# A transformer block's preparation reordered: the condition turned by TensorE, the scale's product before the first turn, key products by part, fillings of zeros regrouped

## The chip, the cores and the metric

The kernel runs on one core of a Trainium2 chip. The metric is the device time of one execution in microseconds. Before the change the median of three runs is 727.88 us (727.65 to 728.49). TensorE (PE) multiplies matrices into PSUM banks; VectorE (DVE), ScalarE (ACT) and GpSimd (POOL) work on tiles of 128 partitions; SyncE (SP) only issues DMA transfers. Each engine takes its instructions in the order in which the program has them and waits on semaphores of the others.

## The reference

The block works on 16 images of 256 tokens with 256 features. A condition vector per image gives shifts, scales and gates; self-attention, cross-attention with a context and an MLP follow, each with a residual.

```python
c_proj = jax.nn.silu(c) @ W_mod + b_mod
shift_a, scale_a, gate_a, shift_m, scale_m, gate_m = jnp.split(c_proj, 6, axis=-1)
x_norm = modulate(_ln(x), shift_a, scale_a)          # t * (1 + scale) + shift
q, k, v = jnp.split(x_norm @ W_qkv + b_qkv, 3, axis=-1)     # 16 heads of 16
attn_w = jax.nn.softmax(jnp.einsum('bhqd,bhkd->bhqk', q, k) * scale, axis=-1)
x = x + gate_a[:, None] * (merge(attn_w @ v) @ W_proj + b_proj)
...                                  # cross-attention with _ln(x) and _ln(context)
h = jax.nn.gelu(modulate(_ln(x), shift_m, scale_m) @ W_mlp1 + b_mlp1)
x = x + gate_m[:, None] * (h @ W_mlp2 + b_mlp2)
```

## The kernel before

The program has 32 *units*: the self-attention (s) of each of the 16 images and its cross-attention (c). For each unit a layernorm `xn` is made, turned by TensorE into feature-major form (`psT`), and multiplied with the weights into keys, queries and values (`ps_k`, `ps_q`, `psv`). Numbers are kept to nearly full float32 by splitting: a value is rounded to the type fp32r (its *high* part, `xTh`, `h_k`, `h_q`) and the rest is kept as a *low* part (`xTl`, `l_k`, `l_q`); a product of two such values is three products, high by high, weight high by low, weight low by high. The helper `mm3` issues these three for each of the two 128-feature halves of the inner dimension, interleaved, so the second of its six instructions already needs the low part. Keys and queries, high twice and low once, are copied by DMA into a *stack* `big` (three buffers, one per unit in flight, one half for queries and one for keys), from which the attention scores are products `st` and `s`. Rows of `big` that no copy writes must be zero; filling them with zeros is one word of the preparation for each half, done by GpSimd (a memset) or by ScalarE (a copy of the zero tile `wz`).

After the attention scores start, a fixed plan of *beats* sets what each engine does next to the two score products. Before it comes the *preparation*, which loads the weights, computes what the condition gives, and brings the first two units through keys and queries. The order of the preparation is written out by hand, as a list of words in the entry `PRE` of the table `E_`; each word is a function that issues instructions on one or more engines, and since every engine keeps program order, the list is the order on every engine. The words that the change and the prediction speak of:

- `load`: the first DMA loads, on SyncE in this order: one block of `W_mod` (for the scale), the bias rows `brow`, the key block of `W_qkv`, the shift's block of `W_mod`, the query block, input `x` of image 1, the value block. The condition `c_sb` is loaded ahead of them, the input of image 0 by ScalarE's queue. `ld2` loads the input of image 2; `lg`, `lc`, `lp` load the gate's, the cross projection's (`wcp_f`) and the projection's (`wp_f`) weights and biases.
- `L0a`, `L0b`, `L0d`: statistics of image 0 (VectorE `st_s`), their aggregate `mv_s` with the root on GpSimd (`rs_s`), and `xn_s` on VectorE. `L1a` to `L1d` are the same for image 1.
- `silu`, `turn`: tanh of half the condition on ScalarE (16 partitions by 256), the product `th` = (tanh + 1) c on VectorE, then TensorE turns `th` and ScalarE halves it into `sT` (128 by 32).
- `scale`, `sc1`, `shift`: eight TensorE instructions each (they show as `st<-sT,wf`), and a bias addition on VectorE into `cpT`; `sc1` adds 1 to the scale.
- `T0t`, `T0h`, `T0l`: the turn of image 0's `xn_s`, its scaled high part on ScalarE (needs `sc1`), its low part on VectorE.
- `brow`, `bp`, `bro2`: the bias rows turned, the odd rows copied on ScalarE and turned, and copied out.
- `hik`, `lok`, `hiq`, `loq`, `hiv`, `lov`: high part of a weight (ScalarE cast into `wself`) and its low part (GpSimd; for v VectorE).
- `K0a`, `K0m`: the first and second six instructions of unit 0's key product. `K0h`, `K0l`: `h_k` and `l_k`. `bk`, `bq`, `bv`: the biases that the shift adds (`st<-cpT,wf`, eight instructions, then `bqkv` on VectorE). `h_k` needs `bqkv`.
- `K0x`, `K0yp`, `K0w` and the same for Q: the three copies into the stack, on SyncE or, with p, on GpSimd's queue.
- `b15` and other `b` with a number: so many 128x128 products of zeros (*fillings* of TensorE, `s<-wz`), two instructions each, whose result nobody reads.
- `z0kp`, `z0qp`, `z1kp`: zeros into the key or query half of buffer 0 or 1 on GpSimd; `z1qa`: on ScalarE. `one0`: two rows of ones into buffer 0 by SyncE.

The first score product (`st<-big`) waits for all six copies of unit 0's stack.

Of the kernel before, what the change touches and what calls it, by code (L numbers as in the profile page):

```python
# [21 lines left out]
def pixart_block(  # L22
# [8 lines left out]
    B, N, H = x.shape  # L31
# [4 lines left out]
    KC = H // P  # L36
# [15 lines left out]
                return tc.keep_in_program_order(i) if self.on else i  # L52
            return issue

    E_ = {'CUT': 8, 'LN': {'s': 'pool', 'c': 'pool', 'q': 'pool'}, 'ON': (1, 1, 1), 'L0': -16, 'L1': 1, 'S0': -7, 'A0': 0, 'T0': 1, 'S1': 5, 'A1': 7, 'L2': 9, 'T1': 9, 'S2': 32, 'AP': 99, 'DV': (0, 1), 'HP': (1, 0), 'BZ': {}, 'AV': {1: [(1, 2), (1, 3)], 9: [(0, 0), (0, 1)]}, 'AHEAD': (0, 0, 0, 0, 0, 2), 'TW': {(21, 6): 'cb', (23, 5): 'u0', (23, 7): 'u1', (25, 2): 'u2', (27, 3): 'u3', (27, 7): 'h2a', (28, 0): 'l2 h0p u5', (28, 2): 'h1p', (28, 4): 'h3p', (28, 7): 'u4 u6', (29, 0): 'l3d', (29, 1): 'l0', (29, 2): 'l1', (29, 7): 'h5p', (30, 1): 'u7 h6d h7p', (30, 3): 'h4p', (31, 1): 'l4 l6d', (31, 2): 'l5d x2', (31, 4): 'l7', (31, 7): 'b2'}, 'BE': 'G0 av P g0 A1 G1 G2 N1 F7 g1 S0 PF s2 p2 G3 a2 aT aL G4 x3 b3 S1 S2 T2 C r0 G5 S3 G6 S4 s3 CF x4 F8 g2 G7 S5 F9 p3 S6 G8 a3 r1 G9 F10 G10 T3 g3 b4 x5 x6 S7 s4 F11 S8 S9 F12 G11 p4 a4 F13 r2 S10 G12', 'XP': 1, 'IL': 1, 'MF': 0, 'SH': 4, 'RAMP': 1, 'HA': 1, 'MP': 16, 'W': (7, 1, 0, 0), 'PRE': 'load L0a z0kp z0qp L0b silu b15 hik turn L0d brow bp z1qa lok T0t lg scale b1 lc sc1 bro2 T0h T0l shift b3 ld2 one0 hiq loq L1a hiv K0a L1b bk K0m L1d bq K0h K0l Q0a L2a T1t T1h lp K0yp K0x z1kp Q0m T1l bv K1a Q0h K0w Q0x Q0yp Q0l lov K1b Q1a Q0w L2b Q1b K1l V0a K1y Q1l z2ka ld3', 'SL': {(-1, 0): 'V0b wm one1 L2c', (-1, 1): 'V1a T2t T2h', (-1, 2): 'K1wp T2p', (-1, 3): 'K1xp L3a Q1yp V1b ga', (-1, 4): 'M0 z2qa Q1xp Q1wp pb L3b vone gs', (-1, 5): 'mods0 ld4', (-1, 6): 'K2a K2m L3p', (-1, 7): 'L3c cb lx gm', (0, 0): 'sp3 mods1', (0, 1): 'sp0', (0, 3): 'sp1', (0, 4): 'sc2', (0, 6): 'one2', (1, 1): 'sp2', (1, 2): 'sp4'}}

    PE = InOrder(nc.tensor, True)
    ACT, DVE, POOL, SP = (InOrder(e, True) for e in (nc.scalar, nc.vector, nc.gpsimd, nc.sync))

    const = ctx.enter_context(tc.tile_pool(name="const", bufs=1))  # L60
    work = ctx.enter_context(tc.tile_pool(name="work", bufs=2))
# [18 lines left out]
    ident = const.tile([P, P], F32, name="ident")  # L80
# [15 lines left out]

    BMOD, BQKV, BKVC, BM1 = 0, 12, 20, 24
    BQ, BK, BQC, BKC = 32, 34, 36, 38
    c_sb, th = [work.tile([B, 2, H], F32, tag=t, name=n, bufs=3)[:, 0] for t, n in (("qkh", "c_sb"), ("qkl", "th"))]
    SP.dma_start(c_sb, cond)  # L100
    X = {}

# [7 lines left out]
    brow = const.tile([32, P], F32, name="brow")  # L110
# [26 lines left out]
    sc1 = const.tile([P, 2, 2, B], F32, name="sc1")  # L137
    bT = const.tile([P, 40], F32, name="bT")
    sT = const.tile([P, KC, B], F32, name="sT")
    cb = const.tile([P, H], F32, name="cb")  # L140
# [43 lines left out]

    def f_silu():
        ACT.activation(dummy, mhalf, AF.Tanh)
        ACT.activation(th, c_sb, AF.Tanh, scale=0.5)
        DVE.scalar_tensor_tensor(th, th, 1.0, c_sb, ALU.add, ALU.mult)

    def f_turn():  # L190
        pst = st[:, 1, 480:]
        for k in range(KC):
            PE.transpose(pst[:, k * B:(k + 1) * B], th[:, k * P:(k + 1) * P], ident[:B, :B])
        ACT.mul(sT.rearrange("p k b -> p (k b)"), pst[:, :KC * B], 0.5)

    odd_rows = []

# [100 lines left out]
    wm = []  # L298
# [9 lines left out]
    gm = []  # L308
# [20 lines left out]
    def layernorm(src, name):  # L329
# [193 lines left out]
    def to_stack(W, src, bias, dst, which, name):  # L523

        o = Box()
        lo_row = (2, 1)[which]

        o.W, o.src, o.tok, o.name = W, src, False, name  # L530

        def first():
            o.ps = ps_gen(f"ps_{name}", LONG)
            mm3(o.ps[:, 0:N], W, 0, src.xT)

        def third():
            mm3(o.ps[:, N:], W, 1, src.xT)

        def second():
            third()  # L540
            high()

        def high():
            o.hi = work.tile([P, KC, N], F32R, tag="qkh", name=f"h_{name}", bufs=3)
            for f in range(KC):
                ACT.activation(o.hi[:, f], o.ps[:, f * N:(f + 1) * N], AF.Identity, bias=bias[f])

        def low():
# [496 lines left out]
    u0, u1 = units[:2]  # L1045
# [17 lines left out]
    for n, v in (("0", u0), ("1", u1), ("2", u2)):  # L1063
        word["T" + n + "t"], word["T" + n + "h"], word["T" + n + "l"] = v.T[0].parts
        word["T" + n + "p"] = v.T[0].low_pool
        for c in "KQ":
            o = getattr(v, c)
            word[c + n + "l"] = o.parts[2]
            word[c + n + "m"], word[c + n + "h"] = o.third, o.high
            word[c + n + "p"] = o.low_pool  # L1070
            for q, k in enumerate("xyw"):
                word[f"{c}{n}{k}"] = lambda o=o, q=q: o.send(q)
                word[f"{c}{n}{k}p"] = lambda o=o, q=q: o.send(q, POOL)
# [20 lines left out]
    u3 = units[3]  # L1094
# [3 lines left out]
    for i in range(5):  # L1098
        word[f"sp{i}"] = lambda i=i: f_split(i)
    word["vone"] = lambda: [POOL.memset(v[:, :, :, HD:], 1.0) for v in vts]  # L1100
    for n, f in (("load", f_load), ("silu", f_silu), ("turn", f_turn), ("brow", f_brow), ("bp", f_bp), ("bro2", f_bro2),
                 ("scale", f_scale), ("sc1", f_sc1), ("shift", f_shift),
                 ("lg", f_loads_g), ("lp", f_loads_p), ("lc", f_loads_c), ("lx", f_loads_x),
                 ("ga", f_ga), ("pb", f_pb), ("gs", f_gs), ("cb", f_cb),
                 ("wm", f_wm), ("mods0", lambda: f_mods(0)), ("mods1", lambda: f_mods(1)), ("sc2", f_sc2), ("gm", f_gm)):
        word[n] = f
# [9 lines left out]
    for i in range(3):  # L1116
        b = i if i < 2 else 0
# [159 lines left out]
    last, o, q = units[-1], units[-1].post, units[-2].post  # L1277
# [103 lines left out]
```

## Time and profile before

| | before |
|---|---|
| median of 3 runs | 727.88 us |
| lowest, highest | 727.65, 728.49 us |
| the profiled execution, its own time | 728.29 us |
| its span, first to last instruction | 726.5 us |
| TensorE busy | 718.9 us, 99% |
| TensorE's share of the chain that ended last | 93% |
| mean granted TensorE clock | 0.997 |

The span is 1.8 us shorter than the execution's own time. Busy time alone doesn't tell what counts: fillings count as busy, and so do products that wait for nothing but are early. The chain of waits is followed back from the last instruction; at each step it goes to what released the instruction or to the one before it on its engine. In rows of engines, the first number is the start in us, the second the duration, then come engine, line, operation, the tiles written and read, their shapes, how many instructions the row holds, and in brackets the idle time before it with what ended it. All recorded operations have the line of the recording helper, L51, so the tiles' names tell them apart.

### The profile page before, as it was taken

The numbers are of one execution on the slowest core, as the hardware profiler recorded it, in microseconds if no ns is written. First come the engines' busy times: TensorE is split into PE (matmuls) and PEld (weight loads), VectorE is DVE, ScalarE is ACT, GpSimd is POOL, SyncE is SP. The second block draws the span as 40 slices with busy tenths as digits, with TensorE's granted clock in tenths as the row PEclk, the third lists the DMA queues.
The fourth block names the chain that finished last, engine by engine and source line by source line (L and its number), as shares of the span: only waits on it lengthen the run. The fifth ranks groups of instructions, "written<-read, shape, count | busy, mean of one in ns | idle before, by whom it ended". The sixth has DMA issues, their size and how long they took to land.

```text
span 726.5 us, 24914 instructions
## 1 busy us (share of the span) xinstructions
PE 718.9 (99%) x10086; PEld 633.3 (87%) x10086; DVE 567.8 (78%) x1208; ACT 579.3 (80%) x1006; POOL 526.8 (73%) x561
## 2 busy tenths in 40 slices
PE   9999999999999999999999999999999999999997
PEld 8788888888888888888888888888878999999997
DVE  4888898989888888888889888888845675676552
ACT  5578898888888888888888888898887677777773
POOL 6766687969687786969687898979746756656643
PEclk9999999999999999999999999999999999999999
DMA  6645333332424343342433444244311414334421
GB/s 208 209 150 176 119 120 143 138 120 105 162 107 161 124 152 124 120 147 112 169 119 137 152 149 161 106 145 142 128 52 54 117 46 117 96 87 111 102 64 39
DMA packets 67110, 90.56 MB, mean 125 GB/s; under 512 B 6194, under 2 KB 38740, under 8 KB 66996
## 3 DMA queue, kind: packets, MB, share of 16 engines
q1 hardware_dynamic: 66164, 86.88, 35.8%
q8 instruction: 80, 1.31, 0.7%
q0 software_dynamic: 560, 1.84, 0.7%
q14 instruction: 34, 0.28, 0.1%
q10 hardware_dynamic: 272, 0.26, 0.1%
HBM read 26.97 MB, written 8.46 MB: 49 GB/s over the span
## 4 chain that ended last, share of the span: by engine, by line
PE 93%; POOL 3%; issue 1%; DVE 1%; ACT 1%; DMA 0%; POOLq 0%; ACTq 0%
PE s L51 18%; PE o L51 16%; PE st L51 15%; PE ph L51 10%; PE ps_P_s L51 4%; PE ps_qc L51 4%; PE ps_v_c L51 4%; PE ps_kc L51 4%; PE ps_q L51 4%; PE ps_v_s L51 3%; PE ps_k L51 3%; PE ps_P_c L51 2%; PE psT_q L51 1%; PE psA_s L51 1%; POOL hl L51 1%
## 5 line engine op out<-in xcount | busy, mean ns | idle before, releaser
L51 DVE TENSOR_REDUCE mx<-s 128x2 f32<-128x512 f32 x504 | 324.7, 683 | 64.3 <-PE s L51 59.0
L51 ACT ACTIVATE pt<-st 128x1024 f32<-128x1024 f32 x252 | 258.9, 1028 | 16.9 <-PE st L51 10.5
L51 PE MATMUL s<-big 63*128 63x256 f32 (+1 forms) x1024 | 185.6, 299 | 0.2
L51 PEld LDWEIGHTS s<-big 63*128 63x128 f32 (+1 forms) x1024 | 133.5, 186 | 19.1 <-DVE l_kc L51 6.6
L51 PE MATMUL st<-big 64*128 64x256 f32 (+1 forms) x1024 | 134.4, 299 | 0.5 <-DMA big<-l_q 0.3
L51 POOL TENSOR_TENSOR hl<-hf,hh 128x512 fp32r<-128x512 f32 x64 | 87.4, 1368 | 63.2 <-ACT hh L51 63.1
L51 PE MATMUL o<-pt,v 128*32 128x256 f32 x2048 | 123.8, 382 | 0.0
L51 PEld LDWEIGHTS st<-big 64*128 64x128 f32 (+1 forms) x1024 | 96.3, 187 | 16.0 <-issue 13.0
L51 PEld LDWEIGHTS o<-pt,v 128*32 128x32 f32 x2048 | 60.0, 109 | 41.4
L51 PE MATMUL ph<-wcross,wself 128*128 128x256 f32 x672 | 85.4, 277 | 0.0
L51 PEld LDWEIGHTS ph<-wcross,wself 128*128 128x128 f32 x672 | 80.4, 188 | 0.0
L51 ACT COPY oT<-o 128x512 f32<-128x512 f32 x63 | 37.0, 587 | 32.7 <-PE o L51 32.7
L51 ACT ACTIVATE hf<-ph,bT 128x256 f32<-128x256 f32 x114 | 47.7, 472 | 18.4 <-PE ph L51 18.4
L51 ACT ACTIVATE hh<-ph,bT 128x256 fp32r<-128x256 f32 x114 | 47.9, 473 | 17.9 <-PE s L51 8.7
L51 PE MATMUL ps_kc<-xTh_c,wcross 64*128 64x256 f32 x256 | 46.6, 291 | 0.0
L51 PE MATMUL s<-big,hh 128*128 128x256 f32 x256 | 45.2, 277 | 0.0
L51 PE MATMUL st<-big,hh 128*128 128x256 f32 x256 | 45.2, 277 | 0.0
L51 PE MATMUL ps_v_c<-wcross,xTh_c 64*128 64x256 f32 x256 | 44.3, 292 | 0.0
L51 PE MATMUL ps_k<-xTh_s,wself 64*128 64x256 f32 (+1 forms) x232 | 43.5, 293 | 0.0
L51 PE MATMUL ps_qc<-xTh_q,wcross 64*128 64x256 f32 x256 | 41.2, 280 | 0.0
L51 PE MATMUL ps_q<-xTh_s,wself 64*128 64x256 f32 (+1 forms) x240 | 40.7, 287 | 0.0
L51 POOL TENSOR_SCALAR xn_c<-c,mv_c,rs_c 128x256 f32<-128x256 f32 x32 | 39.0, 1227 | 1.7
(240 smaller groups left out, 2135.7 us busy)
## 6 DMA issues: line engine op xcount, KB each, us to landing
big<-h_kc SPq DMA_DIRECT2D x32, 256.0 KB
big<-h_qc SPq DMA_DIRECT2D x32, 256.0 KB
big<-h_k SPq DMA_DIRECT2D x30, 256.0 KB
big<-h_q SPq DMA_DIRECT2D x29, 256.0 KB
g<-gd SPq DMA_DIRECT2D x16, 256.0 KB
c<-in_ctx_dram SPq DMA_DIRECT2D x16, 256.0 KB
big<-l_kc SPq DMA_DIRECT2D x16, 256.0 KB
big<-l_qc SPq DMA_DIRECT2D x16, 256.0 KB
```

The source lines that it names most:

```text
L51: i = f(*a, **k)
```

## The change

Four edits, all in the preparation.

1. The condition is turned first: TensorE turns `c_sb` itself, inside `silu`; ScalarE takes from PSUM the tanh of half of it and half of it, both 128 by 32; a new word `th2` multiplies them on VectorE straight into `sT`. `turn` goes.
2. `scale` stands before the turn of image 0 (`T0t`); `shift` behind the first part of the key product.
3. Unit 0's key product is issued by parts: `K0i` all four high-by-high instructions for both output halves, `K0j` the four with the input's low part and then the four with the weight's low part.
4. Fillings: 15 + 1 + 3 products become 5 + 3 + 1 + 1, at other places; the zeros of buffer 0's query half go from GpSimd (`z0qp`) to ScalarE (`z0qa`).

The list moves with it: the load of image 2 goes ahead of the gate's weights, the projection weights (`lc`, `lp`) behind `h_k` and `l_k`, and statistics of image 2 behind `l_q`.

```diff
-    c_sb, th = [work.tile([B, 2, H], F32, tag=t, name=n, bufs=3)[:, 0] for t, n in (("qkh", "c_sb"), ("qkl", "th"))]
+    c_sb, th = [work.tile([p, 2, H], F32, tag=t, name=n, bufs=3)[:, 0]
+                for p, t, n in ((B, "qkh", "c_sb"), (P, "qkl", "th"))]
...
     def f_silu():
         ACT.activation(dummy, mhalf, AF.Tanh)
-        ACT.activation(th, c_sb, AF.Tanh, scale=0.5)
-        DVE.scalar_tensor_tensor(th, th, 1.0, c_sb, ALU.add, ALU.mult)
-
-    def f_turn():
         pst = st[:, 1, 480:]
         for k in range(KC):
-            PE.transpose(pst[:, k * B:(k + 1) * B], th[:, k * P:(k + 1) * P], ident[:B, :B])
-        ACT.mul(sT.rearrange("p k b -> p (k b)"), pst[:, :KC * B], 0.5)
+            PE.transpose(pst[:, k * B:(k + 1) * B], c_sb[:, k * P:(k + 1) * P], ident[:B, :B])
+        ACT.activation(th[:, :KC * B], pst[:, :KC * B], AF.Tanh, scale=0.5)
+        ACT.mul(th[:, KC * B:2 * KC * B], pst[:, :KC * B], 0.5)
+
+    def f_th2():
+        DVE.scalar_tensor_tensor(sT.rearrange("p k b -> p (k b)"), th[:, :KC * B], 1.0, th[:, KC * B:2 * KC * B],
+                                 ALU.add, ALU.mult)
...
+        def some(products):
+            for n, (a, k, f) in enumerate(products):
+                PE.matmul(o.ps[:, f * N:(f + 1) * N], W[a // 2][:, k, f * P:(f + 1) * P], src.xT[a % 2][:, k],
+                          start=(a == n == 0), stop=(a == 2 and k == KC - 1), skip_group_check=True)
+
+        def high_high():
+            o.ps = ps_gen(f"ps_{name}", LONG)
+            some([(0, k, f) for k in range(KC) for f in range(2)])
+
+        def rest():
+            some([(a, k, f) for a in (1, 2) for k in range(KC) for f in range(2)])
+
+        o.by_part = high_high, rest
```

The list `PRE`, before and then after, broken into lines here:

```
load L0a z0kp z0qp L0b silu b15 hik turn L0d brow bp z1qa lok T0t lg scale b1 lc sc1 bro2
T0h T0l shift b3 ld2 one0 hiq loq L1a hiv K0a L1b bk K0m L1d bq K0h K0l Q0a L2a T1t T1h lp
K0yp K0x z1kp Q0m T1l bv K1a Q0h K0w Q0x Q0yp Q0l lov K1b Q1a Q0w L2b Q1b K1l V0a K1y Q1l z2ka ld3
```

```
load z0kp b5 silu L0a th2 L0b z1qa b3 brow bp L0d scale sc1 b1 T0t hik lok T0h bro2 b1 K0i
T0l shift K0j hiq loq ld2 lg one0 z0qa L1a L1b bk L1d K0h hiv K0l Q0a bq K0yp K0x T1t T1h z1kp lc K0w lp
Q0m T1l Q0h bv K1a Q0l Q0x Q0yp lov Q0w L2a K1b Q1a L2b Q1b K1l V0a K1y Q1l z2ka ld3
```

Past the preparation the order on every engine is that of before.

More of the change, by code (lines that the diff above doesn't have):

```diff
@@ new lines, in pixart_block @@
+    E_ = {'CUT': 8, 'LN': {'s': 'pool', 'c': 'pool', 'q': 'pool'}, 'ON': (1, 1, 1), 'L0': -16, 'L1': 1, 'S0': -7, 'A0': 0, 'T0': 1, 'S1': 5, 'A1': 7, 'L2': 9, 'T1': 9, 'S2': 32, 'AP': 99, 'DV': (0, 1), 'HP': (1, 0), 'BZ': {}, 'AV': {1: [(1, 2), (1, 3)], 9: [(0, 0), (0, 1)]}, 'AHEAD': (0, 0, 0, 0, 0, 2), 'TW': {(21, 6): 'cb', (23, 5): 'u0', (23, 7): 'u1', (25, 2): 'u2', (27, 3): 'u3', (27, 7): 'h2a', (28, 0): 'l2 h0p u5', (28, 2): 'h1p', (28, 4): 'h3p', (28, 7): 'u4 u6', (29, 0): 'l3d', (29, 1): 'l0', (29, 2): 'l1', (29, 7): 'h5p', (30, 1): 'u7 h6d h7p', (30, 3): 'h4p', (31, 1): 'l4 l6d', (31, 2): 'l5d x2', (31, 4): 'l7', (31, 7): 'b2'}, 'BE': 'G0 av P g0 A1 G1 G2 N1 F7 g1 S0 PF s2 p2 G3 a2 aT aL G4 x3 b3 S1 S2 T2 C r0 G5 S3 G6 S4 s3 CF x4 F8 g2 G7 S5 F9 p3 S6 G8 a3 r1 G9 F10 G10 T3 g3 b4 x5 x6 S7 s4 F11 S8 S9 F12 G11 p4 a4 F13 r2 S10 G12', 'XP': 1, 'IL': 1, 'MF': 0, 'SH': 4, 'RAMP': 1, 'HA': 1, 'MP': 16, 'W': (7, 1, 0, 0), 'PRE': 'load z0kp b5 silu L0a th2 L0b z1qa b3 brow bp L0d scale sc1 b1 T0t hik lok T0h bro2 b1 K0i T0l shift K0j hiq loq ld2 lg one0 z0qa L1a L1b bk L1d K0h hiv K0l Q0a bq K0yp K0x T1t T1h z1kp lc K0w lp Q0m T1l Q0h bv K1a Q0l Q0x Q0yp lov Q0w L2a K1b Q1a L2b Q1b K1l V0a K1y Q1l z2ka ld3', 'SL': {(-1, 0): 'V0b wm one1 L2c', (-1, 1): 'V1a T2t T2h', (-1, 2): 'K1wp T2p', (-1, 3): 'K1xp L3a Q1yp V1b ga', (-1, 4): 'M0 z2qa Q1xp Q1wp pb L3b vone gs', (-1, 5): 'mods0 ld4', (-1, 6): 'K2a K2m L3p', (-1, 7): 'L3c cb lx gm', (0, 0): 'sp3 mods1', (0, 1): 'sp0', (0, 3): 'sp1', (0, 4): 'sc2', (0, 6): 'one2', (1, 1): 'sp2', (1, 2): 'sp4'}}
@@ L1068, in pixart_block @@
             word[c + n + "l"] = o.parts[2]
+            word[c + n + "i"], word[c + n + "j"] = o.by_part
             word[c + n + "m"], word[c + n + "h"] = o.third, o.high
@@ L1100, in pixart_block @@
     word["vone"] = lambda: [POOL.memset(v[:, :, :, HD:], 1.0) for v in vts]
-    for n, f in (("load", f_load), ("silu", f_silu), ("turn", f_turn), ("brow", f_brow), ("bp", f_bp), ("bro2", f_bro2),
+    for n, f in (("load", f_load), ("silu", f_silu), ("th2", f_th2), ("brow", f_brow), ("bp", f_bp), ("bro2", f_bro2),
                  ("scale", f_scale), ("sc1", f_sc1), ("shift", f_shift),
```

1 line of the change is left out of this document (removed).

## The prediction

> **What bounds the kernel now.** I read the page's busy table first, then the chain of waits, then each engine's timeline of the first 22 us, which is all that the change touches.
>
> ```profile
> span 726.5 us, 24914 instructions
> PE 718.9 (99%) x10086; PEld 633.3 (87%) x10086; DVE 567.8 (78%) x1208; ACT 579.3 (80%) x1006; POOL 526.8 (73%) x561
> ```
>
> TensorE is busy for 99% of the span, so once its work is dense nothing but its own work sets the end. What is left is the time until it is dense. The chain of waits of the first 22 us (start, duration, what):
>
> ```profile
> 1.85 3.49 POOL big L51 x2
> ...
> 5.42 0.24 POOL rs_s L51
> 5.73 0.72 POOL rs_s L51
> ...
> 6.48 0.43 DVE xn_s L51
> 6.96 0.87 PE psT_s L51 x4
> 7.83 0.80 PE st L51 x8
> ...
> 9.18 0.99 PE st L51 x8
> 10.18 0.76 PE s L51 x6
> 10.94 0.95 PE ps_k L51 x6
> 11.88 0.84 PE st L51 x8
> 12.73 0.80 PE ps_k L51 x6
> 13.53 0.84 PE st L51 x8
> 14.37 0.81 PE ps_q L51 x6
> 15.18 0.45 PE psT_s L51 x4
> ...
> 17.49 0.79 DVE l_q L51 x2
> 18.30 2.69 DMA big<-l_q
> 21.13 0.50 PE st L51 x4
> ```
>
> Three things are to be seen. Two fillings of `big` on GpSimd hold the first layernorm's `rs_s` until 5.42. From 7.83 to 10.94 TensorE does preparation products (`st`) and fillings (`s`): it is busy, but the unit's first product waits. The chain leaves this stage at 21.13, when the last part of the first stack, `l_q`, has landed. From there TensorE has work queued in order, so I price the change by how much earlier the row at 21.13 comes.
>
> **The change part by part.** ScalarE and VectorE show what the first product waits for (engine, operation, idle time before it in brackets):
>
> ```profile
> 3.18 0.41 ACT L51 ACTIVATE th<-c_sb 16x256 f32<-16x256 f32 x1 [0.47 <-DMA c_sb<-in_cond_dram]
> 3.81 0.75 DVE L51 BATCH_NORM_STATS2 st_s<-x 128x6 f32<-128x256 f32 x2 [2.56 <-DMA x<-in_x_dram]
> 4.48 0.30 DVE L51 BATCH_NORM_AGGREGATE mv_s<-st_s 128x2 f32<-128x6 f32 x2
> 8.73 0.19 DVE L51 TENSOR_TENSOR cpT<-st,bT 128x32 f32<-128x32 f32 x1 [1.51 <-PE st L51]
> 6.29 0.66 ACT L51 CAST wself<-wf 128x512 fp32r<-128x512 f32 x1 [2.70 <-DMA wf<-in_L_xcond_W_qkv_dram]
> 6.86 0.18 ACT L51 ACTIVATE sT<-st 128x32 f32<-128x32 f32 x1
> 7.34 1.89 ACT L51 CAST big<-wz 128x2048 fp32r<-128x2048 f32 x1
> 9.58 0.84 ACT L51 ACTIVATE xTh_s<-psT_s,sc 128x256 fp32r<-128x256 f32 x2
> 10.45 0.88 DVE L51 SCALAR_TENSOR_TENSOR xTl_s<-psT_s,sc,xTh_s 128x256 fp32r<-128x256 f32 x2 [1.08 <-ACT xTh_s L51]
> 13.57 0.84 ACT L51 ACTIVATE h_k<-ps_k,bqkv 128x256 fp32r<-128x256 f32 x2 [2.07 <-PE ps_k L51]
> 15.65 0.84 ACT L51 ACTIVATE xTh_s<-psT_s,sc 128x256 fp32r<-128x256 f32 x2 [1.25 <-PE psT_s L51]
> 17.41 0.87 DVE L51 SCALAR_TENSOR_TENSOR l_q<-ps_q,bqkv,h_q 128x256 fp32r<-128x256 f32 x2
> ```
>
> *Condition and fillings.* `sT` was made at 6.86, after ScalarE's `wself` cast that waited for a load until 6.29. Now TensorE turns the raw condition as soon as it lands (3.18, the wait that ScalarE's `th` had; only fillings are queued behind it on TensorE), and ScalarE's tanh and half (0.18 each by the `sT` row, estimated, the operation being of the same size) come before that cast. `x` arrives at 3.81, so VectorE's new `sT` product stands behind the statistics: 3.81 + 0.67 = 4.48, then about 0.19 (the `cpT` row). `sT` is ready at 4.7 instead of 7.04. The statistics end 0.18 later, at 4.9. GpSimd has one filling of 1.75 instead of two, so it is free by 3.6; `rs_s` starts at 4.95 instead of 5.42. Gain: 0.45. The other filling goes to ScalarE, which after `xTh_s` (to 8.25, below) and a weight cast (0.66) has nothing until `h_k` at 11.75; the filling takes 1.89. Ten of the first filling instructions go; their time is TensorE time that waited for `xn_s` anyway, so nothing, unless the clock below minds.
>
> *Scale before the turn.* The eight `st` products (0.80) plus `cpT` and `sc` now run from 4.9 to 5.8, beside GpSimd's `rs_s`. No row shows when their weights land: they are second in SyncE's queue, so after `c_sb` (3.18) and before the weight that the cast waited for (6.29). At 6.29 the turn would wait 0.7; one transfer behind `x` at 3.81 is 4.5, and I take no delay. VectorE's `cpT` and `sc` follow `xn_s`, from 6.7 to 7.1. The turn `psT_s` starts at 6.5 and ends 0.87 later, at 7.4. ScalarE's cast of zeros (1.89) starts at 4.0 and the cast of the first weight (0.66, from 6.3) ends at 6.95, so `xTh_s` starts at 7.4 instead of 9.58: 2.15 earlier. This is the main gain: 0.45 of it from GpSimd, 1.7 from what stood between turn and `xTh_s`.
>
> *High products first.* On TensorE, before and then in the change, from the first turn of the input to the key's bias (`bk`, the `st` of `cpT`):
>
> ```order
> L51 MATMUL psT_s_161<-ident,xn_s_152 128x128 x4
> L51 MATMUL st<-sT,wf_104 128x16 x4
> L51 MATMUL s_102<-wz 128x128
> L51 MATMUL s_103<-ident,bp 128x32 x2
> L51 MATMUL st<-sT,wf_104 128x16 x4
> L51 MATMUL s_102<-wz 128x128 x3
> L51 MATMUL ps_k_209<-xTh_s_185,wself 128x256
> L51 MATMUL ps_k_209<-xTl_s_186,wself 128x256
> ```
>
> ```order
> L51 MATMUL st<-sT,wf_104 128x16 x4
> L51 MATMUL s_102<-wz 128x128
> L51 MATMUL psT_s_158<-ident,xn_s_148 128x128 x4
> L51 MATMUL s_103<-ident,bp 128x32 x2
> L51 MATMUL s_102<-wz 128x128
> L51 MATMUL ps_k_174<-xTh_s_165,wself 128x256 x4
> L51 MATMUL st<-sT,wf_104 128x16 x4
> L51 MATMUL ps_k_174<-xTl_s_166,wself 128x256 x4
> L51 MATMUL ps_k_174<-xTh_s_165,wself 128x256 x4
> L51 MATMUL st<-cpT,wf_105 128x16 x4
> ```
>
> The `st` product that moved from before the fillings to between the key products is the shift. It used to lie in the wait for `xTl_s`; now it starts when the second half of `xTh_s` is there, 8.3. TensorE then has two high products (0.23), shift (0.99), eight key products (0.95) and `bk` (0.90, between 0.84 and 0.99): 8.3 + 3.1 = 11.4, and with `bqkv` (0.19) and hand-overs `h_k` starts at 11.75, 1.8 before 13.57. The whole key product is now ahead of `bk`, so what follows (`ps_q` 0.81, `st` 0.84, first turn of unit 1) begins at 11.4 and the turn ends at 13.6 against 15.63. `xTh_s` of unit 1 follows, then `h_q`, `xTl_s`, `l_q` in the order of before: `l_q` at 15.4 instead of 17.41. Gain up to here: 2.0.
>
> *The stack's transfers.* SyncE's queue, before and then in the change:
>
> ```order
> L51 DMA wcp_f<-in_L_xcond_W_cproj_dram 128x2x256
> L51 DMA bc<-in_L_xcond_b_cproj_dram 1x256
> L51 DMA x_199<-in_x_dram 128x2x256
> L51 DMA big<-ones 1x8x256 x2
> L51 DMA wp_f<-in_L_xcond_W_proj_dram 128x2x256
> L51 DMA gb<-in_L_xcond_b_proj_dram 16x256
> L51 DMA big<-h_k_241 32x4x512
> ```
>
> ```order
> L51 DMA big<-ones 1x8x256 x2
> L51 DMA big<-h_k_222 32x4x512
> L51 DMA wcp_f<-in_L_xcond_W_cproj_dram 128x2x256
> L51 DMA bc<-in_L_xcond_b_cproj_dram 1x256
> L51 DMA big<-l_k_226 32x4x512
> L51 DMA wp_f<-in_L_xcond_W_proj_dram 128x2x256
> ```
>
> Two loads of 256 KB now stand behind `h_k`'s wait, and among the stack's six transfers of 256 KB. But they fill the DMA engines. The rates from 12 to 22 us, in 40 slices, and three later rows of the chain:
>
> ```profile
> GB/s 37 16 0 0 0 0 0 0 66 0 0 0 0 0 16 377 344 320 434 360 320 377 393 205 0 49 352 369 410 377 393 295 393 393 115 197 369 385 180 176
> 28.05 1.04 PE ps_pb L51 x4
> ...
> 30.95 1.57 PE ps_k L51 x12
> ...
> 37.74 1.30 PE ps_q L51 x12
> ```
>
> Nobody misses the two loads early: `ps_pb`, the first to use one, runs at 28.05. At about 370 GB/s a transfer takes 0.71 us. Before, the engines emptied between `h_k`, `l_k` and `h_q` (slices of 0 to 205). With eight transfers from 13.9 on (`h_k` ends at 12.6, and before data moved from slice 15, 15.75, 1.3 after `h_k` had ended), a full queue ends at 13.9 + 8 x 0.71 = 19.6. Without a backlog `l_q` is issued at 16.3 and lands 2.69 later, at 19.0. So the first `st` comes at 19.1 to 19.7 instead of 21.13; TensorE is there before (turn 13.45, `ps_q` 0.81, `st` 0.84, and 30 products at 0.12, between the 0.108 and 0.131 of the last two rows: 18.7). Gain 1.4 to 2.0; I take 1.7, between the two, since the loads are the only ones and sit ahead of `l_q`.
>
> *Sum.* 2.0 at `l_q` less 0.3 of backlog is 1.7. The profiled run took 728.29 (span 726.5 and 1.8 around it); 1.7 less is 726.6. The median of the three runs is 0.4 lower, 727.88, and the forecast on that scale is **726.2 us**.
>
> **The clock.** One thing can undo this. The granted clock, TensorE alone, in stretches of 3.41 us counted back from where it changed (busy us, products, clock, DMA share, GB/s), and what TensorE did in the second of them:
>
> ```profile
> 8.31:11.72 3.41, 3.41 (x27) 1.00 0.99 309
> 35.61:39.03 3.42, 3.24 (x32) 1.00 0.67 230
> 39.03:42.44 3.41, 3.41 (x39) 0.50 0.63 243
> L51 PE MATMUL s<-big 63*128 63x256 f32 x8 | 1.7, 342 | 0.0
> L51 PE MATMUL ps_q<-xTh_s,wself 64*128 64x256 f32 x8 | 1.1, 277 | 0.0
> ```
>
> For 3.41 us the clock was halved, after a stretch in which TensorE looks busy but works on 63 or 64 of 128 rows. Weighing each product by rows and columns, that stretch holds 24 products of 256 columns at 0.12 on half the rows (`s`, `ps_q` and four `st`), 0.42 of its time, and eight of 16 columns; 8.31 to 11.72 has eight fillings and six `ps_k`, 14 x 0.12 or 0.49, and kept its clock. So a stretch at about 0.4 can lose it (an estimate from one event). The new order's 4.89 to 8.31 holds four fillings, four turns and three key products, 11 x 0.12 = 1.3 us, or 0.39. A halved 8.31 to 11.72 lies on the path throughout and costs about 1.5 (at most 1.71).
>
> The Trainium skill (TensorE: Matmul & The Clock Gate, "Why this matters for your kernels") names idle gaps above about 3 us between bursts of products as what brings the half clock back. By that rule the new order's idle, under 1 us, would cost nothing and the sum above stands; the trace does not agree, since TensorE was idle 0.18 us in the stretch before the half clock.
>
> **The rivals.** That nothing moves is none: the order shows the moves.
> - *A cold stretch early, the late one staying.* For it: 0.39 against 0.42. Against: one event is a thin base, and the next stretch up that kept its clock is 0.49. Gain 1.7 - 1.5 = 0.2: **727.7**.
> - *The late cold stretch goes, none comes.* The work of 35.6 to 39.0 moves 1.7 us on the grid. Gain 1.7 + 1.5: **724.7**. If one goes and an early one comes, the forecast stands.
> - *Slower: thin stretches twice.* The work from 27.00 (`st`, `psm`, a wait for `m`, `ps_pb`, `s`, `ps_mods`) counts about 0.45 (12 products on half the rows, `psm`, four `ps_pb` at twice 0.12) if one stretch of the grid falls on it; moved, one may. An early cold stretch and this one, with the late one kept, cost 3.0: 728.3 + 1.3 on the profiled scale, **729.2** on the median's. It decides once two stretches more than now lose their clock.
> - *The backlog is worse.* `h_q` and `l_q` each wait a further transfer, 0.7: gain 1.0, **726.9**.
>
> **How the numbers follow.** A measurement here can tell 0.2%, 1.46 us, from no change; faster means under 726.42. Forecast 0.50, its own range 725.8 to 726.6 (the two landings), four fifths of it under 726.42; early cold stretch 0.28; late one gone 0.13; backlog 0.04; slower 0.05. Faster: 0.40 + 0.13, and a little of the neighbours, 0.54. Same: 0.40. Slower: 0.06. The range 724.5 to 728.0 takes in the early and the vanished cold stretch and leaves out the slow rival and the tails.
>
> **What would show it.** Right: `xTh_s` near 7.4, `h_k` near 11.8, `l_q` near 15.4 to 16.3, the first `st` of the stack at 19.1 to 19.7, and from there the rows of before 1.4 to 2.0 earlier. Granted clock 0.50 from 8.3 would show the first rival; none at all, the second; a landing of `l_q` after 19.9, the backlog. Wrong: `xTh_s` at 7.4 but the first `st` still past 20.5 at full clock, or the gain lost again after 22 us.

## The result, and the profile after

The changed kernel is slower: 734.66 us median of 7 runs (731.52 to 739.34) against 727.88 (727.28 to 728.49, 7 runs of before beside it), a ratio of 1.0085 with a 95% interval of 1.006 to 1.011. The forecast was 726.2, in a range of 724.5 to 728.0.

The profiled execution took 731.52, the least of the seven; the six others took 734.49 and more. So there are two losses to find: about 3 us that the profile shows (its span is 729.7, before 726.5), and about 3 us more, in the others, that it does not show. The page after:

```profile
span 729.7 us, 24878 instructions
...
PE 720.0 (99%) x10068; PEld 634.1 (87%) x10068; DVE 568.3 (78%) x1208; ACT 581.5 (80%) x1007; POOL 526.5 (72%) x560
```

The timelines of ScalarE and VectorE, with the four rows that the prediction had put at 7.4, 11.75, 13.6 and 15.4:

```profile
7.31 0.84 ACT L51 ACTIVATE xTh_s<-psT_s,sc 128x256 fp32r<-128x256 f32 x2 [0.39 <-PE psT_s L51]
...
11.73 0.84 ACT L51 ACTIVATE h_k<-ps_k,bqkv 128x256 fp32r<-128x256 f32 x2 [0.90 <-DVE bqkv L51]
...
13.56 0.84 ACT L51 ACTIVATE xTh_s<-psT_s,sc 128x256 fp32r<-128x256 f32 x2 [0.48 <-PE psT_s L51]
...
15.32 0.87 DVE L51 SCALAR_TENSOR_TENSOR l_q<-ps_q,bqkv,h_q 128x256 fp32r<-128x256 f32 x2
```

Up to there the change does in this execution what was said, to a tenth of a microsecond. The chain of waits goes on:

```profile
15.40 0.78 DVE l_q L51 x2
...
18.18 3.50 DMA big<-h_k
21.67 0.54 PE st L51
```

The first score product starts at 21.67, not at 19.1 to 19.7, and 0.54 after the 21.13 of before. The lead of 2.1 us at `l_q` is gone within one wait. The view puts the wait down to the copy issued last, `h_k` of the next unit at 18.18, which the product does not read; the landing events of the trace have `h_q` at 20.77 and `l_q` at 21.43, and it is `l_q` that the product needs last. (A copy lands in 16 parts; these are the times of the last one.) SyncE's queue after the change (start and length of the issue):

```profile
12.59 0.65 SPq L51 DMA_DIRECT2D big<-h_k  x1
13.29 0.59 SPq L51 DMA_DIRECT2D wcp_f<-in_L_xcond_W_cproj_dram  x1
13.92 0.36 SPq L51 DMA_DIRECT2D bc<-in_L_xcond_b_cproj_dram  x1
14.39 0.78 SPq L51 DMA_DIRECT2D big<-l_k  x1
15.21 0.61 SPq L51 DMA_DIRECT2D wp_f<-in_L_xcond_W_proj_dram  x1
15.87 0.90 SPq L51 DMA_DIRECT2D gb<-in_L_xcond_b_proj_dram  x1
16.86 0.54 SPq L51 DMA_DIRECT2D big<-h_q  x1
17.50 0.58 SPq L51 DMA_DIRECT2D big<-l_q  x1
```

and before:

```profile
17.28 0.53 SPq L51 DMA_DIRECT2D big<-h_q  x1
18.30 0.53 SPq L51 DMA_DIRECT2D big<-l_q  x1
```

`l_q` is ready at 16.19 and issued at 17.50, since the loads with their issues of 0.4 to 0.9 stand ahead of it; from issue to landing it takes 3.9 instead of 2.69. TensorE alone, in stretches of 3.41 us counted from where its granted clock changed (busy us and products, clock, DMA share, GB/s). In every trace here the times at half clock between the first full clock and the end of the work last 3.41 us or a multiple of it (6.83, 17.07, 20.48), so in each execution the stretches form a fixed grid:

```profile
4.61:8.02 3.41, 3.41 (x24) 1.00 0.95 314
...
14.85:18.26 3.41, 3.41 (x31) 1.00 0.97 308
18.26:21.68 3.41, 0.34 (x5) 1.00 1.01 336
21.68:25.09 3.41, 3.41 (x16) 0.50 1.00 297
25.09:28.50 3.41, 3.41 (x19) 0.50 0.17 60
...
38.75:42.16 3.41, 3.23 (x32) 1.00 0.78 231
42.16:45.57 3.41, 3.41 (x38) 0.50 0.64 242
```

The DMA engines are full from 14.85 to 25.09. TensorE is all but idle from 18.26 to 21.68 and then has half its clock for 6.8 us. Set beside the same ScalarE instructions of before, the profiled execution is 2.2 us ahead at 18.7, 2.9 behind at 27.2, 3.3 behind at 31 and 3.2 behind at the end. The late half-clock stretch of before (39.03 to 42.44) is still there, at 42.16. That explains the profiled execution, not the six others.

### The profile page after: what moved, and what is told of

The parts are those of the page before. It is cut to its first block, busy times and chain, and to the rows that moved or that the text cites. A ratio compares the mean times of both kernels' runs of the same rounds, so it can differ in the third digit from the quotient of the medians.

```text
span 729.7 us, 24878 instructions
## 1 busy us (share of the span) xinstructions
PE 720.0 (99%) x10068; PEld 634.1 (87%) x10068; DVE 568.3 (78%) x1208; ACT 581.5 (80%) x1007; POOL 526.5 (72%) x560
## 4 chain that ended last, share of the span: by engine, by line
PE 95%; POOL 1%; DVE 1%; issue 1%; ACT 1%; DMA 0%; POOLq 0%
PE s L51 18%; PE st L51 16%; PE o L51 16%; PE ph L51 10%; PE ps_qc L51 5%; PE ps_q L51 4%; PE ps_P_s L51 4%; PE ps_kc L51 3%; PE ps_k L51 3%; PE ps_v_c L51 3%; PE ps_v_s L51 3%; PE ps_P_c L51 2%; PE psT_q L51 1%; PE ps_h L51 1%; PE psA_s L51 1%
```

## The experiments

Every kernel was timed beside the kernel before on the same chip. Runs of before in these rounds have medians of 728.2 to 728.8; about one in five of them took over 731. The ratio is taken over the runs as a whole and is not the quotient of the two medians; the two differ where the times fall into groups.

**The changed kernel again**, unchanged, for a second profile.

> The changed kernel once more, for a second trace: six of its seven runs took about 734.7 us and only the profiled one 731.5. Theory 1 (the two projection loads share the DMA engines with the first stack, so l_q lands 0.8 us after the time of before instead of 2 us ahead of it, TensorE idles 3 us and its clock is halved): the first stack's product at 21 to 22 us again, and where the run takes 734 to 735, more stretches at half clock after it than the two of the first trace. Theory 2 (the new order of TensorE's own work, with fewer fillings, loses the clock whatever the transfers do): half clock already before 18 us in the slower runs.

734.23 median (730.71 to 735.12, 8 runs), ratio 1.0063 (1.0036 to 1.0089). This time the profile fell on an execution of 734.37, like most. Its rows of TensorE's timeline:

```profile
3.79 1.65 PE L51 MATMUL s<-wz 128*128 128x128 f32 x6
...
9.70 1.20 PE L51 MATMUL ps_k<-xTh_s,wself 128*128 128x256 f32 x4
10.69 1.72 PE L51 MATMUL st<-sT,wf 128*128 128x16 f32 x8
...
28.14 0.50 PE L51 MATMUL st<-big 63*128 63x256 f32 x4
```

and those of the first profile of the same program:

```profile
3.80 1.31 PE L51 MATMUL s<-wz 128*128 128x128 f32 x6
...
7.84 0.88 PE L51 MATMUL ps_k<-xTh_s,wself 128*128 128x256 f32 x4
8.55 0.96 PE L51 MATMUL st<-sT,wf 128*128 128x16 f32 x8
```

Eight `st` products take 1.72 against 0.96: TensorE has half its clock. The first record of its clock in this trace says full from 27.008 on. So it had half its clock through the whole preparation, and the first score product comes at 28.14, 7.0 after that of before, with no wait ahead of it. The view by stretches doesn't show this: it counts the time ahead of the first record as full clock, and so does the mean clock, which is 1.0 for this execution and for the five others of its kind here. The number of products tells it:

```profile
9.94:13.36 3.41, 3.41 (x18) 1.00 0.04 11
...
27.01:30.42 3.41, 3.41 (x28) 1.00 0.80 255
```

In the two rounds 11 of 15 runs of this program lie at 734.2 to 735.1, three at 730.7 to 733.2 and one at 739.3. The second loss is a clock that is granted at 27 us instead of at 4.6: shown in one profile, and taken over to the runs of the same time and the same mean clock.

**The loads ahead of the stack again**, in the changed kernel.

```diff
-... ld2 lg one0 ... z1kp lc K0w lp Q0m ...
+... ld2 lg lc lp one0 ... z1kp K0w Q0m ...
```

> The changed kernel with one thing undone: the loads of the two projection weights and their biases stand behind the gate's loads again, ahead of the first stack. Theory 1: l_q lands about 2.7 us after its issue at 16.2, the first stack's product at 19 to 19.5, no half clock at 21.7, total 725.5 to 726.6, faster than before. Theory 2: the stack's product also comes early, but the total stays at 731 to 735 with half clock in the preparation.

729.06 median (726.07 to 734.69, 10 runs), ratio 1.0006 (0.9967 to 1.0045). The profiled execution, 728.54, from SyncE's queue and TensorE's timeline:

```profile
16.20 0.53 SPq L51 DMA_DIRECT2D big<-l_q  x1
```

```profile
19.91 0.50 PE L51 MATMUL st<-big 63*128 63x256 f32 x4 [1.24 <-DMA big<-l_q]
```

`l_q` is issued as soon as it is ready, and the first score product comes 1.76 earlier than with the loads among the copies. It is 0.2 to 0.8 later than the forecast's 19.1 to 19.7, since `l_q` still needed 3.6 to land (19.78). By the landing events 15 of its 16 parts were there at 18.85, 2.65 after the issue and so as fast as before; the last part came 0.93 behind them. Before, all 16 came within 0.14. What held the one part, no view shows. A stretch with 1.24 us of idle then lost the clock once:

```profile
18.48:21.89 3.41, 2.17 (x17) 1.00 0.78 242
21.89:25.30 3.41, 3.41 (x19) 0.50 0.73 238
```

The median misses what was expected (725.5 to 726.6), since the ten times fall apart: three of 726.07 to 726.44 with a mean clock of 1.0, three of 728.54 to 729.26 with 0.994 or 0.995 (the kind profiled), and four of 734.3 to 734.7, as slow as with the loads late. So the loads cost what the first profile shows where the clock is granted early. In executions that have half their clock through the preparation they cost nothing: there the first score product of the changed kernel had no wait, with the loads late. The three best are where the prediction put the change, 726.2.

**The same loads moved in the kernel before**: late, as in the change, and nothing else.

```diff
-... b1 lc sc1 ... T1h lp K0yp K0x z1kp ... K0w Q0x ...
+... b1 sc1 ... T1h K0yp K0x lc z1kp ... K0w lp Q0x ...
```

> The kernel before with one part of the change alone: the loads of the two projection weights and their biases moved behind the first copies of the key, as the change has them. Theory 1: l_q lands 2 us or more later than 21.0, TensorE idles 2 to 3 us and loses its clock, total 731 to 735. Theory 2: at most the delay itself, under 1 us, total 728 to 729.

731.95 median (729.73 to 733.71, 10 runs), ratio 1.0034 (1.0009 to 1.0059). `l_q` is issued at 18.82 instead of 18.30, and TensorE's timeline and stretches have the same picture:

```profile
23.56 0.50 PE L51 MATMUL st<-big 63*128 63x256 f32 x4 [2.79 <-DMA big<-h_k]
```

```profile
22.07:25.48 3.41, 1.92 (x15) 1.00 1.01 327
25.48:28.89 3.41, 3.41 (x19) 0.50 0.48 172
```

The loads alone, in the old preparation, put the first score product 2.43 later and cost 3.5 us in the median (2.5 by the ratio). No run of these ten lies at 734: this part does not make the late clock.

**Fillings where TensorE waits for the stack**, fourteen pairs at the end of the changed preparation (the word is `b14`, two instructions a pair).

```diff
-... z2ka ld3
+... z2ka ld3 b14
```

> The changed kernel with 14 more products of zeros (28 instructions, about 3.1 us) on TensorE ahead of the first stack's product, where it idled 3.1 us. Transfers are as in the changed kernel. Theory 1: the product still comes at about 21.7, but the clock stays full behind it: what the half clock cost (about 2.8 us in the first trace, more in the slower runs) comes back, total 727.5 to 729. Theory 2: no change against the changed kernel within 1 us, 731 to 735.

734.25 median (727.81 to 737.63, 10 runs), ratio 1.0062 (1.002 to 1.0104). Five runs lie at 737.2 to 737.6, the profiled one among them, with a first clock record at 27.09; the fillings, which then fill no wait, come on top. The other five lie at 727.8 to 731.3 where the changed kernel has 730.7 to 733.2: their mean clock is 0.996 to 0.999 where that of the changed kernel is 0.992 to 0.995, so there the fillings seem to keep the clock that the wait had lost (none of the five was profiled). The fillings do nothing for the late clock.

**Fillings for fillings**: in the changed kernel ten pairs for three behind the condition's turn. TensorE is given full-size products from 1.04 to 6.5 and beyond, as before, but for the turn in between.

```diff
-load z0kp b5 silu L0a th2 L0b z1qa b3 brow ...
+load z0kp b5 silu L0a th2 L0b z1qa b10 brow ...
```

> The changed kernel with fourteen fillings more behind the turn of the condition (`b3` becomes `b10`), so that fillings run from 1.04 to about 6.5 as they did before; the two loads stay among the stack's copies. Theory A (the regrouped fillings no longer fill one whole 3.41 us window in most runs, and TensorE then has half its clock until 27 us): the runs near 734.5 go, all or nearly all lie at 730 to 733, as the changed kernel's one profiled run with an early full clock (731.5), less nothing for the scale's product, which comes up to 1 us later. Rival B (the late clock has nothing to do with the fillings but with the order of the products behind them, st and the turn ahead of the first key product): at least half of the runs stay near 734.5 or come later by the fillings' length, 735.5. Rival C (the loads alone cost the 6 us): median stays at 734.

734.04 median (733.18 to 738.25, 12 runs), ratio 1.0069 (1.0045 to 1.0092). The time missed what was expected of theory A (730 to 733) and by itself fits the rivals B and C. The clock tells against B: every mean clock is 0.991 to 0.995, not 1.0, so by the mean each run was granted its full clock early and lost it again for a while, and the profiled execution has its full clock from 7.257. Against C speaks the next kernel. But the fillings are long at half clock, and the rest queues behind them:

```profile
3.80 4.13 PE L51 MATMUL s<-wz 128*128 128x128 f32 x20
...
11.23 0.88 PE L51 MATMUL ps_k<-xTh_s,wself 128*128 128x256 f32 x4 [0.72 <-ACT xTh_s L51]
```

The first key product starts at 11.23 instead of 7.84; with the loads still late, the first score product came at 24.91 after 2.93 of idle, and the clock was lost for two more stretches (24.32 to 31.15).

**The same with the loads early.**

```diff
-... b10 brow ... ld2 lg one0 ... z1kp lc K0w lp Q0m ...
+... b10 brow ... ld2 lg lc lp one0 ... z1kp K0w Q0m ...
```

> The same fillings and also the two loads ahead of the stack's copies (`lc lp` behind `lg`). Theory A with the loads as a second effect: no runs near 734.5; the runs lie at 726 to 729.5, median near 727, those with the lowest time at 726.1 as in the kernel with the loads alone moved, since first `st` starts near 19.9 again or up to 1 us later where the clock is granted late in the fillings. Rival B: 4 of 10 runs near 734.5 or above, as in the kernel with the loads alone moved.

728.51 median (727.7 to 734.09, 12 runs), ratio 1.0012 (0.9984 to 1.004). Eight runs lie at 727.7 to 728.7 with a mean clock of 1.0, four at 733.5 to 734.1 with 0.991. The profiled one (728.29) has its full clock from 6.465 and keeps it; the first score product starts at 22.09, a microsecond later than before the change. So the fillings buy the early clock and pay for it with the head start. The four were not expected by theory A and are about as many as rival B expected; but their mean clock is not the 1.0 of the runs with a late clock, so by the mean they are of another kind, of which there is no profile.

**The fillings alone, cut in the kernel before**: eight pairs for fifteen.

```diff
-load L0a z0kp z0qp L0b silu b15 hik turn ...
+load L0a z0kp z0qp L0b silu b8 hik turn ...
```

> The kernel before with eight filling pairs for fifteen ahead of the silu's turn (`b15` becomes `b8`, 16 instructions that end near 4.4), and nothing else. Theory A: TensorE then idles until the turn at about 6.5, and in most runs (three of four by the windows that still fit) has no full clock in the preparation: those runs take 734 to 737, the others 727.5 to 729; median near 735. Rival B (the fillings do not matter, the order of the new preparation does): median 728, as before.

734.48 median (731.69 to 736.76, 12 runs), ratio 1.0055 (1.0029 to 1.0082); no run near 728. Fewer fillings, and nothing else, cost the old preparation 6 us in the median (4 by the ratio). Five of the runs have a mean clock of 0.999 or 1.0 and lie at 734.1 to 734.7, where most runs of the change lie: with half its clock TensorE has no idle time in the preparation (none from 3.79 to 27.01 in the second profile above), so a shorter order on the other engines would gain nothing there. The profiled execution (736.76), in stretches:

```profile
0.52:3.93 3.41, 2.89 (x13) 1.00 0.57 173
3.93:7.34 3.41, 1.26 (x10) 1.00 0.81 237
7.34:10.76 3.41, 3.41 (x16) 0.50 1.02 340
...
24.41:27.82 3.41, 3.41 (x17) 0.50 0.61 233
27.82:31.24 3.42, 3.42 (x29) 1.00 0.43 138
```

Here the clock was granted at 3.93 and lost at 7.34, after a stretch in which TensorE waited, and it came back at 27.82 alone. From 10.76 to 27.82 TensorE was never idle by these rows (3.41 of 3.41), and still it did not come back for 17 us.

**Six pairs more ahead of the stack**, on top of fillings and early loads.

```diff
-... z2ka ld3
+... z2ka ld3 b6
```

> As the kernel with the fillings and the loads both put back, with six filling pairs more at the end of the preparation, where TensorE waits 1.2 us for `l_q`. Theory A: runs at 725.8 to 727.5, median near 726.3; the half-clock stretch at 21.9 to 25.3 goes, and with it the runs at 728.5 to 729.3. Rival (idle ahead of the stack has no part in that stretch): median as without the six, 727.

730.11 median (729.88 to 735.98, 11 runs), ratio 1.0031 (1.0 to 1.0063): missed. With the long fillings TensorE waits only 0.40 for `l_q`; twelve fillings of 1.5 us delay the first score product to 22.92. Eight runs are within 0.6 of each other, but 1.7 above most of those without the six pairs. The later product (22.92 for 22.09) is half of that; the profiled run also has half its clock from 40.76 to 44.17, which the profiled one without the six pairs has not.

**Fewer fillings, with early loads**: six pairs behind the condition's turn.

```diff
-load z0kp b5 silu L0a th2 L0b z1qa b10 brow ...
+load z0kp b5 silu L0a th2 L0b z1qa b6 brow ...
```

> The changed kernel with the two loads ahead of the stack's copies and six filling pairs behind the condition's turn in place of three (`b3` becomes `b6`; ten pairs were too many: they ended at 7.55 at half clock and put the first key product from 7.84 to 10.85). Theory A: where the 3.41 us window ends near 6.5, fillings to about 6.3 are enough for a full clock from there, at a delay of 0.4 to 1 us for the scale's product: most runs at 726.2 to 729, median near 727.5; those whose window ends near 3.9 and 7.3 stay without (733 to 735), 1 to 3 of 10. Rival (a full window needs the long uninterrupted filling of before, the condition's turn at 3.5 breaks it): 4 of 10 near 734.5 as with three pairs.

734.52 median (726.37 to 735.92, 12 runs), ratio 1.003 (0.9993 to 1.0068). Five runs lie at 726.4 to 728.2 and seven at 734.4 to 735.9: more than the 1 to 3 of 10 of theory A and no fewer than the rival's 4 of 10. Five of the seven have a mean clock of 0.988 and not 1.0, so by the mean they had been granted it early and lost it, as in the kernel before with eight pairs (0.986 in its profile).

**Seven pairs ahead of the turn and five behind it.**

```diff
-load z0kp b5 silu L0a th2 L0b z1qa b6 brow ...
+load z0kp b7 silu L0a th2 L0b z1qa b5 brow ...
```

> The same with seven pairs ahead of the condition's turn and five behind it (`b5` becomes `b7`, `b3` becomes `b5`): the turn stands 0.55 us later on TensorE, at about 4.0, still before the scale's product could start. Theory A: a window that ends at 3.93 is now also filled from 1.04 (85% of it, as in the kernel before with eight pairs, which got its full clock at 3.93): 0 to 2 of 10 runs above 732, the rest at 726.5 to 729.5, median near 727.5. If the clock granted at 3.93 is lost again at 7.34, as it was there, 2 to 3 of 10 stay at 733 to 735.

727.55 median (725.72 to 735.31, 12 runs), ratio 0.9982 (0.9949 to 1.0015). Nine runs at 725.7 to 728.1, three at 734.8 to 735.3 with a mean clock of 0.988. One of the three was profiled:

```profile
3.14:6.55 3.41, 3.41 (x17) 1.00 0.83 261
6.55:9.97 3.41, 2.96 (x22) 1.00 1.06 352
9.97:13.38 3.41, 3.16 (x15) 0.50 0.53 165
```

Granted at 6.55, lost at 9.97, after a stretch that has 22 instructions and 0.45 us of idle, but eight of the 22 are `st` products of 16 columns, and three only turn bias rows.

**That stretch filled**: four pairs for one in the wait for `xTh_s`.

```diff
-... T0h bro2 b1 K0i ...
+... T0h bro2 b4 K0i ...
```

> As the kernel with seven and five pairs, with four filling pairs for one behind the turn of the input (`b1` ahead of the first key products becomes `b4`), where TensorE waited 0.71 us for `xTh_s`. There the one profiled run lost its clock at 9.966, after a stretch (6.55 to 9.97) with seven fillings and four turns, 11 x 0.11 or 0.35 of it. Theory A (a stretch with too little full-size work loses the clock): six fillings more make 17 x 0.11 or 0.55 of that stretch, the clock stays, and the runs near 735 (3 of 12) go or fall to 1 of 12; the rest as there, 725.7 to 728.2; median 727, below the kernel before by 1 to 1.5. Rival (those runs lose their clock for the wait itself or for another reason): 3 of 12 near 735 or above stay.

726.82 median (726.25 to 728.06, 12 runs), ratio 0.9981 (0.997 to 0.9993): faster than the kernel before, by 1.3 us, and 7.4 to 7.8 below the changed one's two medians. No run lies above 728.1. Three runs of twelve near 735 and then none are few to tell the theories apart; the next kernel, with the same four pairs, has none of that kind in twelve either. The 0.2% is that of the best of several variants and was not measured a second time. The profiled execution in stretches:

```profile
2.36:5.78 3.41, 3.41 (x17) 1.00 0.86 268
5.78:9.19 3.41, 3.41 (x28) 1.00 0.99 324
...
39.91:43.32 3.41, 3.28 (x51) 1.00 0.35 133
```

and its chain of waits at the stack:

```profile
18.22 2.67 DMA big<-l_q
20.89 0.14 issue
21.02 0.50 PE st L51 x4
```

It is no faster to the first score product than the kernel before (21.02 against 21.13). It is 0.1 ahead at 27.7 and 1.04 at 54: it has no half-clock stretch at 39 to 42, which the profiled execution of before has. So between these two profiles the gain is clock, not preparation. It is not the whole account of the median: the runs of before in this round that have a mean clock of 1.0 have a median of 727.7, still 0.9 above, and no trace shows why.

**One pair fewer behind the condition's turn.**

```diff
-... z1qa b5 brow ... bro2 b4 K0i ...
+... z1qa b4 brow ... bro2 b4 K0i ...
```

> As the last, with four pairs for five behind the condition's turn, so that the scale's product can start 0.2 to 0.4 us earlier. Theory A: the best runs are 0.1 to 0.4 faster, 725.4 to 725.8, if windows that end near 6.5 are still filled enough (fillings to about 6.3 at half clock); if not, 3 to 5 of 12 runs come at 733 to 736.

727.11 median (725.82 to 730.59, 12 runs), ratio 0.9989 (0.9969 to 1.001). Five runs lie at 725.8 to 726.2, just above what was hoped for (725.4 to 725.8), and four at 730.3 to 730.6; the profiled one of these has its first full clock at 13.756. With eight fillings for ten behind the turn, the stretch that ended at 6.93 got it no clock (0.70 in the table below); whether ten would have, in that place of the grid, no trace shows.

**What the clock goes by.** The traces together allow an estimate. In each stretch of 3.41 us I counted how much of it was full-size work: 0.213 us at half clock (the starts of the ten fillings from 1.04 stand 0.213 apart) and half of that, 0.107, at full clock, for a filling, a turn or a product of 256 columns; an eighth of that for an `st` of 16 columns; and all of it in proportion to the rows used of 128. Ahead of the first record the clock is taken as half, as the lengths of the products there have it. The weights were chosen after the runs, so the table describes these traces and is no test.

| stretch, of which execution | share of full-size work | clock in it, and then |
|---|---|---|
| 10.34:13.76, seven, four and four pairs | 0.78 | half, full |
| 0.52:3.93, before with eight pairs | 0.81 | half, full |
| 3.14:6.55, seven and five pairs | 0.81 | half, full |
| 1.20:4.61, the change, first profile | 0.81 | half, full |
| 23.59:27.01, the change, second profile | 1.00 | half, full |
| 3.52:6.93, seven, four and four pairs | 0.70 | half, half |
| 0.43:3.84, the change with ten pairs | 0.69 | half, half |
| six stretches from 3.12 to 23.59, the change, second profile | 0.48 to 0.59 | half, half |
| 6.55:9.97, seven and five pairs | 0.32 | full, half |
| 35.61:39.03, before | 0.40 | full, half |
| 38.75:42.16, the change, first profile | 0.36 | full, half |
| 4.61:8.02, the change, first profile | 0.38 | full, full |
| 8.31:11.72, before | 0.47 | full, full |

In all 14 traces the first grant comes after a stretch of 0.78 or more, and none of at most 0.70 at half clock was followed by one. For losing it the bound is less sharp: stretches of 0.40 and less were followed by half clock or not. Where the grid of stretches stands differs from one execution to the next: the first stretch to end after 2 us ends at 2.4 in one of these traces, and in others at 3.1, 3.5, 3.9, 4.6 or 5.2. By the estimate fifteen pairs without a break, as before, cover a stretch for most places of the grid; ten fillings, the condition's turn and six fillings cover one for few.

## Why the prediction was wrong

*`xTh_s` 7.4, `h_k` 11.75, the turn of unit 1 at 13.6, `l_q` 15.4.* Right in the change's first profile, where the clock is granted early: 7.31, 11.73, 13.56, 15.32. Gains and their order, condition first, scale ahead, high products first, were as reckoned (the turn of unit 1 ends at 13.53; the prediction has it at 13.6 in one sum and at 13.45 in another). In most executions none of it holds, for the reason that comes third.

*"I take 1.7, between the two, since the loads are the only ones and sit ahead of `l_q`"*, a backlog of 0.3. This is the term that was mis-sized. The backlog was reckoned as eight transfers at the full rate, with a landing of `l_q` at 19.0 to 19.6. It landed at 21.43, and with the loads early, where no backlog was reckoned, near 19.8. Three things were left out: the issues themselves, which put `l_q` on the queue 1.3 after it was ready; the transfers issued behind it from 18.18 on, unit 1's `h_k` first, which move at the same time (by 21.43 the engines had moved 2.43 MB, 9.3 transfers of 256 KB and not eight, at 323 GB/s from 13.9 on and not 370); and that an `l_q` 1.8 late costs TensorE an idle stretch and then the clock, 6.8 us at half. The prediction priced a late landing at its own length; the loads cost 3.5 us in the old preparation's median. Its own sign of being wrong, `xTh_s` at 7.4 but the first `st` past 20.5, is what the first profile shows. The rival with the worse backlog (726.9) had the place right and the price wrong in the same way.

*"Ten of the first filling instructions go; their time is TensorE time that waited for `xn_s` anyway, so nothing, unless the clock below minds."* This step failed, and with it the sign. TensorE's first fillings, before and then in the change (six more follow from 3.80):

```profile
1.04 5.44 PE L51 MATMUL s<-wz 128*128 128x128 f32 x30 [1.04 <-DVE wz L51]
```

```profile
1.04 2.50 PE L51 MATMUL s<-wz 128*128 128x128 f32 x10 [1.04 <-DVE wz L51]
```

Thirty instructions became sixteen, so fourteen went and not ten. They were nobody's input; what they did was to get the clock granted. Cut in the kernel before, they cost 6 us in the median by themselves; put back in the change they end the runs with a clock from 27 us.

*The clock.* That a stretch with little full-size work is dangerous was right, and that TensorE's idle time does not tell. But the section looked for a lost clock at 8.31 to 11.72, with a price of 1.5, and took the clock's start for given, since before it was full from 4.9. The stretch of 0.39 that it feared (here 4.61 to 8.02) kept the clock. What fell was the first grant, for which more is needed (0.78) than for keeping it. One trace of before showed one place of the grid; the argument had it that the grid would stand there again. By the rule that the prediction quoted from the Trainium skill (TensorE: Matmul & The Clock Gate, "Why this matters for your kernels"), idle gaps above about 3 us bring the half clock back. The 3.1 us at 18.59 agrees; the 1.24 us ahead of 19.91 and the stretches with 0.18 and 0.45 us of idle do not. The Trainium skill (TensorE: Matmul & The Clock Gate, "What's actually happening") has the throttled state as the default and the window as free-running, "it doesn't reset when your kernel starts". The runs bear that out (first grants at 3.93 to 7.26, 13.76 and 27.0 to 27.1 us, at half clock until then), and this rule spoke against the change: a first window that is not busy at its place in the grid is followed by another at half clock.

*The rivals.* The slower one (729.2, chance 0.05) had thin stretches past the first; the place was wrong and the chance too small. The late half-clock stretch stayed in the change's first profile, as the forecast had it.

*What is left open.* Why a stretch at 0.30 to 0.40 sometimes keeps the clock and sometimes not; the estimate counts columns and rows, and may leave out something that the clock goes by. How often each place of the grid comes was not measured either, beyond the groups of times. The run of 739.34 was not explained, nor were the runs of before above 731, of which none was profiled.

## What to carry to other kernels

Products that nobody reads may be what holds the clock: before cutting or splitting fillings at a kernel's start, ask whether full-size products still cover four fifths (the estimate above) of a 3.41 us window wherever that window falls, and take a second and third profile, since one shows one place of the grid. Keep loads out of a queue between copies that the next stage waits for, and price a late landing with the clock that the idle engine loses, not with its length alone. When a preparation gets shorter, its fillings have to be laid anew around it: here that, with the loads early, was worth more than 7 us and turned a loss of 0.8% into a gain of 0.2%.

## What the runs showed that was not expected

- TensorE busy without a break for 23 us at half clock (3.79 to 27.01 in the second profile of the change): products of 16 columns, eight at a time, keep an engine busy and the share of full-size work at 0.48 to 0.59.
- Granting and losing have different bounds, about 0.75 and about 0.4 by the estimate above.
- The mean granted clock of an execution that had half its clock for 27 us reads 1.0, above the 0.992 of one that had it from 4.6 on. What tells them apart is the length of equal products: eight `st` in 1.72 or 0.96 us.
- The copy of `l_q`, 256 KB, took 2.69 from issue to landing with idle times between the copies, and 3.93 with other loads in flight and the engines full. With the loads early it took 3.58, of which 0.93 is one of its 16 parts behind the other 15.
